# ScalarE copies in layer 0's norms and transforms, and expert inputs prepared two pairs ahead, in a four-layer network

## The chip, the cores and the metric

The kernel runs on one core of one Trainium2 chip. The metric is the device time of one execution in microseconds (us). A core has five engines that each work through their own queue of instructions in order: TensorE (PE: matrix products, with its weight loads shown as PEld), VectorE (DVE), ScalarE (ACT), GpSimd (POOL) and SyncE (SP, which here issues most DMA transfers). They wait for one another by semaphores. Matrix products land in PSUM, in banks of 128 x 512 floats, and an engine other than PE has to read a bank before PE can use it again.

## The reference

Eight samples of 256 channels and 32 x 32 pixels, all in float32, pass through four layers. The parts that the change touches are these:

```python
# layer 0, all of it on (B, 256, 32, 32)
def _ln(x, w, b):                       # the norm ahead of attention and of the feed-forward part
    r = lax.rsqrt(jnp.mean(x * x, axis=1, keepdims=True) + LN_EPS)
    return x * r * w + b
a = _attention(_ln(x, norm1_w, norm1_b), ...)   # softmax attention, 4 heads, plus a depthwise 3x3 of v
x = x + gamma1 * a
f = _edffn(_ln(x, norm2_w, norm2_b), ...)       # 1x1 (pi), depthwise 3x3, gelu(x1) * x2, 1x1 (po),
x = x + gamma2 * f                              # then rfft2 of 8x8 patches * fft_p, irfft2
# layer 1: a bottleneck with a deformable 3x3 convolution
# layer 2: causal attention; then a feed-forward part for the 511 tokens of 1024 with the largest weight
weights = x @ wr + br
_, idx = top_k(weights, 512);  sel = x[idx[:511]]
y = (gelu(sel @ w1 + b1) @ w2 + b2) * weights[sel];  out = x, with y added at the picked rows
# layer 3: attention with squared scores in place of a softmax; then 8 experts, two for each token
probs = softmax(tokens @ router_w.T);  rw, re = top_k(probs, 2)
for e in range(8):
    out += combine[:, e] * (gelu(tokens @ w1[e] + b1[e]) @ w2[e] + b2[e])
```

## The kernel before, in words

**Layers and order.** Six generators, `fast0` to `fast3e` (list LAYERS), give the instructions of layer 0, layer 1, layer 2's attention, layer 2's feed-forward part, layer 3's attention with routing, and layer 3's experts. They run one after the other; each one's first steps are drawn in at the end of the one before by `net.head()`. Inside a layer several streams, one for each sample and stage, are merged by `by_time`: every stream has a start and a spacing in steps, and the one that is due next gives its next step. `spread` does the like in layer 3. A scheduler then may reorder the instructions of an engine where data allow it; an instruction that goes through `net.pinned` keeps its place in program order. Each engine's queue runs in order on the chip, so an instruction that waits holds back everything behind it on its engine.

**Layer 0** (`fast0`, L1110). The main stream is attention, 32 steps a sample (T = 32): a step makes scores s on PE (L1393), exponentials e of 128 x 1024 on ScalarE (L1399), values A on PE (L1357) and the running sum of e on DVE (L1353). Beside it run, for other samples: `before_attention` (norm, q, k, v, depthwise part of v), `before_gates` (the second norm), `gates` (the 1x1 pi, L78 through `net.linear`; its copies to hp by ScalarE, L1434; the depthwise 3x3 as eight DVE steps of about 1.23 us each, L1246; gelu on ScalarE between two loads of its function table, L1459 and L1460) and `transforms` (po, fwd, gain, back: L1487 to L1507, four times a sample). All of these take their PSUM from `bank`, which while attention runs has two banks (tag X) in rotation: PE can use a bank when the engine that reads the one of two before has done so. After attention there are four.

`normed` (L1213) is called twice a sample. For each of the two halves k of the channels ScalarE squares 128 x 1024 (L1218) and PE sums the square over channels into a bank ms (L1220); in `before_gates` both squares use one buffer `sq`, so the second square waits for the first product. ScalarE makes r = rsqrt (L93, L94), PE spreads r over all partitions into two banks rb (L1229), and DVE multiplies x by each of the banks (L1233, 128 x 1024 each). In `transforms`, fwd (L1495) is multiplied by the gain on DVE out of PSUM (L1496).

**Layer 2's feed-forward part** (`fast2f`, L2044). `before(b)` makes the norm xn of a sample by ScalarE, then on DVE eight products with wr (L2116) that yield the column wcol, and an added constant (L2119). PE turns wcol into a row wrow (L2124) by which the tokens are ranked. `place` scatters tokens, `ready` loads the picked ones and turns them (xs, L2178; copied by DVE to xk, L2183), `main` makes h (L78), its gelu, and y (L2200), to which DVE adds b2 (L2207). The DVE instructions L2119 and L2207 are not pinned; in the engine's order, from the third sample on, an addition L2207 of an earlier sample stands between the fifth and the sixth product L2116.

**Layer 3's attention and routing** (`fast3`, `Routes`). `between(b)` runs beside sample b's attention: it routes sample b - 1 and makes the norm and projections of sample b + 1. For b = 0 it first runs `routes.fill`: DVE makes a row of zeros with a destination that is out of bounds, and eight DMAs on SP's queue (L2359) write such rows to the three lists into which tokens will be sorted by expert.

**Experts** (`fast3e`, L2725). The lists are worked in 76 pairs of blocks of 128 rows, in three groups. For pair q: `load` fetches rows xs by DMA, four pairs ahead, into five buffers; `fetch` turns xs on PE (a, L2807) and copies it by DVE to xk (L2809, two buffers); `first` makes h on PE (L2821) and its gelu hid (L2827); `second` converts the rows' destinations (`to`, L2839, POOL, pinned), makes y on PE (L2843), adds b2 on DVE (L2847) and scatters each block by POOL (L1026). Step q issues `first(q)`, `fetch(q + 1)`, `second(q - 1)`. Beside it, `sort` prepares the last group and `combine` adds up the results of finished groups (L2909) and turns them back (oT, L2920).

Of the kernel before, what the change touches and what calls it, by code (L numbers as in the profile page):

```python
# [17 lines left out]
P = 128  # L18
# [1091 lines left out]
def fast0(net, io):  # L1110
# [7 lines left out]
    with ExitStack() as ctx, ExitStack() as att:  # L1118
# [94 lines left out]
        def normed(xn, x, sq):  # L1213

            ps = bank("ms")
            for k in range(KC):
                s_ = sq(k)
                nc.scalar.activation(s_, x[:, k, :], AF.Square)  # L1218
                for h in range(2):
                    nc.tensor.matmul(  # L1220
                        ps[64 * h : 64 * h + 64], lhsT=net.mean64, rhs=s_[:, bass.ts(h, HF)],
                        start=(k == 0), stop=(k == KC - 1),
                    )
            r = one.tile([P, HF], F32, tag="r", name="r")
            net.rsqrt(r, ps, net.eps6)
            yield
            for h in range(2):
                pr = bank("rb")
                nc.tensor.matmul(  # L1229
                    pr, lhsT=net.unit[64 * h : 64 * h + 1, :], rhs=r[64 * h : 64 * h + 1, :], start=True, stop=True  # L1230
                )
                cols = bass.ts(h, HF)
                nc.vector.tensor_tensor(  # L1233
                    xn[:, :, cols], x[:, :, cols], pr.unsqueeze(1).to_broadcast([P, KC, HF]), ALU.mult
                )
# [183 lines left out]
        def before_gates(b):  # L1419
            xn = xs[b] = one.tile([P, KC, N], F32, tag="xn2", name="xn2")  # L1420
            nc.sync.dma_start(out=xn, in_=mids[b])
            yield
            yield from normed(xn, xn, lambda k: one.tile([P, N], F32, tag="sq", name="sq"))
            yield
# [42 lines left out]
        def transforms(b):  # L1467
# [12 lines left out]
            for pr in range(4):  # L1480
# [4 lines left out]
                for pc in range(2):  # L1485
# [10 lines left out]
                nc.vector.tensor_tensor(  # L1496
                    u, ps.rearrange("p (t c) -> p t c", c=C), gain.unsqueeze(1).to_broadcast([P, 2, C]), ALU.mult
                )
# [19 lines left out]
        for b in range(B):  # L1518
            streams += [
                (T * (b - 1) - 2, 32 / 20, before_attention(b)) if b > 1 else (11 * b, 1.0, before_attention(b)),  # L1520
                (T * (b + 1) + 7.5, 1, before_gates(b)),
# [3 lines left out]
        for _ in range(9):  # L1525
            next(streams[1][2])
# [517 lines left out]
def fast2f(net, io):  # L2044
# [5 lines left out]
    with ExitStack() as ctx, ExitStack() as mid:  # L2050
# [26 lines left out]
        def before(b):  # L2077
# [41 lines left out]
            nc.vector.tensor_scalar(wcol, wcol, vec[:, 10:11], None, ALU.add)  # L2119
# [66 lines left out]
        def main(b):  # L2186
# [9 lines left out]
            for t2 in range(0, 4, 2):  # L2196
                ps = bank("y")
                for i in range(2):
# [8 lines left out]
                nc.vector.tensor_tensor(  # L2207
                    y[:, t2 : t2 + 2], ps.rearrange("p (t c) -> p t c", c=C),
                    b2.unsqueeze(1).to_broadcast([P, 2, C]), ALU.add,
# [86 lines left out]
class Routes:  # L2296
# [49 lines left out]
    def fill(self):  # L2346
# [8 lines left out]
        for g, so in enumerate(self.sorteds):  # L2355
            self.fills[g] = []
            for lo in range(0, TILES[g], 26):
# [4 lines left out]
                )  # L2362
                self.fills[g].append(ins.ins)
# [142 lines left out]
def fast3(net, io):  # L2506
# [4 lines left out]
    with ExitStack() as ctx, ExitStack() as tok, ExitStack() as att, ExitStack() as bef:  # L2511
# [175 lines left out]
        def between(b):  # L2687

            if b:
                yield from routes.route(b - 1, xs[b - 1], one, pair)  # L2690
            else:
                yield from routes.fill()
            if b + 1 < B:
                yield from norm(b + 1)
                yield from projections(b + 1)
            else:
# [28 lines left out]
def fast3e(net, io):  # L2725
# [4 lines left out]
    with ExitStack() as ctx:  # L2730
# [9 lines left out]
        five = io.pool(ctx, "f3ec", 5)  # L2740
        psP = io.pool(ctx, "f3ep", 1, PSUM)
# [26 lines left out]
        def experts():  # L2768
            xss, xks, w1s, hids = {}, {}, {}, {}
# [28 lines left out]
            def fetch(q):  # L2798
# [5 lines left out]
                xs, ps = xss[q], bank("a")  # L2804
# [3 lines left out]
                xks[q] = two.tile([P, 2, KC, P], F32, tag="xk", name="xk")  # L2808
                nc.vector.tensor_copy(  # L2809
                    xks[q][:, :n].rearrange("p j k n -> p (j k n)"), ps[:, :n].rearrange("p j c -> p (j c)")  # L2810
                )

# [19 lines left out]
            def second(q):  # L2832
# [4 lines left out]
                hid, xs = hids.pop(q), xss.pop(q)  # L2837
                to = five.tile([P, 2], I32, tag="to", name="to")
                net.pinned(nc.gpsimd.tensor_copy(to[:, :n], xs[:, :n, C]))  # L2839
# [19 lines left out]
            fetch(0)  # L2859
            yield  # L2860
            for q in range(len(pairs)):
# [3 lines left out]
                fetch(q + 1)  # L2865
# [73 lines left out]
        sorting = sum(steps[:-1]) - lead - 2 * AHEAD - 2  # L2939
# [281 lines left out]
```

## Time and profile before

| what | value |
|---|---|
| time, median of three runs (lowest, highest) | 4359.39 us (4353.24, 4366.02) |
| the profiled execution's own time | 4372.2 us |
| its span in the trace | 4370.4 us |
| its mean granted clock of TensorE | 0.948 |
| busy: PE, DVE, ACT, POOL | 4008.9, 2298.0, 2228.2, 564.7 us |
| busy, weight loads (beside PE) | 1944.2 us |
| DMA | 350.34 MB, 80 GB/s in the mean |

A row of the waits names the engine, its operation and line, what ended the idle time before it, and then the total in us, the number and the longest. A row of the timeline has start and duration in us, engine, line, operation, out<-in with partitions x elements, how many such instructions are merged (x), and in brackets the idle time just before the first and what ended it; "issue" and "remote" stand where the profile shows no releasing instruction. A row of stages has the stretch in us, its length, the busy time of each engine with the number of instructions, the granted clock of TensorE (1 is full speed), the DMA engines' busy share and GB/s. The stages in the span are, roughly: layer 0 to 1480, layer 1 to 1950, layer 2's attention to 2450, its feed-forward part to 2980, layer 3's attention to 3960, the experts to 4335, and the last sums to the end.

### The profile page before, as it was taken

The numbers are of one execution on the slowest core, as the hardware profiler recorded it, in microseconds if no ns is written. First come the engines' busy times: TensorE is split into PE (matmuls) and PEld (weight loads), VectorE is DVE, ScalarE is ACT, GpSimd is POOL, SyncE is SP. The second block draws the span as 40 slices with busy tenths as digits, with TensorE's granted clock in tenths as the row PEclk, the third lists the DMA queues.
The fourth block names the chain that finished last, engine by engine and source line by source line (L and its number), as shares of the span: only waits on it lengthen the run. The fifth ranks groups of instructions, "written<-read, shape, count | busy, mean of one in ns | idle before, by whom it ended". The sixth has DMA issues, their size and how long they took to land. (4 is left out here: it accounts for less than half of the span.)

```text
span 4370.4 us, 53086 instructions
## 1 busy us (share of the span) xinstructions
PE 4008.9 (92%) x20006; PEld 1944.2 (44%) x20006; DVE 2298.0 (53%) x3995; ACT 2228.2 (51%) x2966; POOL 564.7 (13%) x645
## 2 busy tenths in 40 slices
PE   8989999999888889989999988889999999998887
PEld 3223333333333444444444435554444444336776
DVE  2387877887886577752222246642332323324345
ACT  3455555555453366643433454425665556665444
POOL 0000000000000000000000013331000150134653
PEclk9988999999898999999999988899999999999998
DMA  2212222222213111110100012346100040145566
GB/s 89 67 59 84 88 74 89 86 76 80 79 47 116 62 42 58 40 43 1 39 20 20 29 48 93 118 145 186 37 30 30 20 127 30 35 132 179 186 211 212
DMA packets 190636, 350.34 MB, mean 80 GB/s; under 512 B 24121, under 2 KB 134668, under 8 KB 178852
## 3 DMA queue, kind: packets, MB, share of 16 engines
q1 hardware_dynamic: 167124, 294.10, 20.8%
q0 software_dynamic: 19440, 46.45, 3.2%
q10 hardware_dynamic: 3808, 6.29, 0.4%
q8 instruction: 162, 2.65, 0.3%
q14 instruction: 102, 0.84, 0.1%
HBM read 175.15 MB, written 153.89 MB: 75 GB/s over the span
## 5 line engine op out<-in xcount | busy, mean ns | idle before, releaser
L1246 DVE SCALAR_TENSOR_TENSOR a<-hp,w_f_vec,a 128x961 f32<-128x961 f32 (+1 forms) x496 | 608.5, 1232 | 154.3 <-ACT a L1239 146.2
L2677 ACT ACTIVATE e<-s,five 128x1024 f32<-128x1024 f32 x512 | 539.2, 1110 | 276.9 <-PE s L2671 260.6
L2671 PE MATMUL s<-q,k 32*128 32x512 f32 x2048 | 349.2, 645 | 7.9 <-DVE cnt L2437 2.0
L78 PE MATMUL pi<-xn,w_l_wpi 128*128 128x512 f32 x512 | 268.1, 670 | 41.5 <-DVE u L1496 31.0
L1399 ACT ACTIVATE e<-s 128x1024 f32<-128x1024 f32 x256 | 249.3, 1020 | 109.0 <-PE s L1393 106.3
L2655 PE MATMUL A<-e,v 128*32 128x512 f32 x2048 | 279.6, 611 | 0.3 <-ACT e L2677 0.3
L1353 DVE TENSOR_TENSOR sum<-sum,e 128x1024 f32<-128x1024 f32 x192 | 230.7, 1218 | 87.6 <-ACT e L1399 87.5
L1357 PE MATMUL A<-e,va 128*32 128x512 f32 x2048 | 268.8, 606 | 0.0
L1434 ACT ACTIVATE hp<-pi,pib 128x512 f32<-128x512 f32 x128 | 87.6, 688 | 229.5 <-PE pi L78 223.4
L1393 PE MATMUL s<-q,k 32*128 32x512 f32 x1024 | 199.4, 664 | 0.2 <-ACT e L1399 0.2
L2821 PE MATMUL h<-xk,w 128*128 128x128 f32 x1192 | 159.2, 290 | 43.1 <-DVE xk L2809 33.7
L78 PEld LDWEIGHTS pi<-xn,w_l_wpi 128*128 128x128 f32 x512 | 104.6, 214 | 199.0 <-issue 118.7
L2671 PEld LDWEIGHTS s<-q,k 32*128 32x128 f32 x2048 | 111.2, 184 | 173.7 <-issue 99.2
L2821 PEld LDWEIGHTS h<-xk,w 128*128 128x128 f32 x1192 | 153.1, 204 | 54.9 <-DVE xk L2809 38.9
L1721 PE MATMUL pos<-pos,w_f_sel 64*128 64x512 f32 x576 | 163.6, 629 | 9.3 <-ACT ax L1732 2.9
L1026 POOL DMA_INDIRECT res<-y,to x149 | 150.1, 1007 | 153.3 <-issue 135.2
L2792 ACT COPY w<-w_l3f_w 128x512 f32 x149 | 92.6, 625 | 138.3 <-PE h L2821 107.3
L1307 POOL MEMSET thrice<- 32x128 f32 x32 | 6.3, 196 | 1085.0 <-PE pe L1324 1062.3
L2843 PE MATMUL y<-w_l3f_w,hid 128*128 x596 | 143.0, 382 | 0.2 <-ACT hid L2827 0.2
L1026 POOL DMA_INDIRECT so<-xl,rows x128 | 129.6, 1012 | 91.7 <-issue 62.0
L1357 PEld LDWEIGHTS A<-e,va 128*32 128x32 f32 x2048 | 58.8, 110 | 175.6 <-issue 175.6
L2584 DVE COPY v<-v 128x1024 f32<-128x1024 f32 x16 | 19.5, 1223 | 217.0 <-PE v L78 217.0
(404 smaller groups left out, 7149.8 us busy)
## 6 DMA issues: line engine op xcount, KB each, us to landing
x<-d SPq DMA_DIRECT2D x31, 1024.0 KB
xs<-so SPq DMA_DIRECT2D x73, 260.0 KB
so<-zero SPq DMA_DIRECT2D x5, 3380.0 KB
thrice<-v SPq DMA_DIRECT2D x256, 64.0 KB
gated<-st SPq DMA_DIRECT2D x32, 512.0 KB
hc<-gated SPq DMA_DIRECT2D x32, 512.0 KB
d<-x SPq DMA_DIRECT2D x16, 1024.0 KB
xl<-mox SPq DMA_DIRECT2D x64, 256.0 KB
```

Source lines behind the costliest of these rows:

```text
L78: self.nc.tensor.matmul(ps, lhsT=w[:, i, m], rhs=src[:, i, cols], start=(i == 0), stop=(i == k - 1))
L1026: made = self.nc.gpsimd.indirect_dma_start(**args)
L1246: nc.vector.scalar_tensor_tensor(to, fr, taps(t_), to, ALU.mult, ALU.add)
L1353: nc.vector.tensor_tensor(half, half, e[j], ALU.add)
L1357: nc.tensor.matmul(state["A"][32 * h : 32 * h + 32, c, :], lhsT=vas[b][:, kt, c, 32 * h : 32 * h + 32], rhs=e[h // 2][:, h % 2, :], start= ...
L1393: nc.tensor.matmul(ss[h // 2][:, h % 2], lhsT=ks[b][32 * h : 32 * h + 32, bass.ts(kt, P)], rhs=qs[b][32 * h : 32 * h + 32, bass.ts(gq, HF) ...
L1399: nc.scalar.activation(es[i][j], ss[j], AF.Exp, scale=SCALE)
L1721: nc.tensor.matmul(ps[:, bass.ts(h, HF)], lhsT=sel[r, t, xy, :], rhs=poss[b][r, :], start=True, stop=True)
L2655: nc.tensor.matmul(A[32 * h : 32 * h + 32], lhsT=v[:, kt, c * P + 32 * h : c * P + 32 * h + 32], rhs=e[:, h, :], start=first, stop=last,)
L2671: nc.tensor.matmul(ss[h // 2][:, h % 2], lhsT=k[32 * h : 32 * h + 32, c, bass.ts(kt, P)], rhs=q[32 * h : 32 * h + 32, c, bass.ts(hh, HF)], ...
L2677: nc.scalar.activation(e[:, 2 * j : 2 * j + 2], ss[j], AF.Square, scale=SCALE, bias=five)
L2821: nc.tensor.matmul(ps[:, j, m], lhsT=ws[j][:, k, bass.ts(m, P)], rhs=xk[:, j, k], start=(k == 0), stop=(k == KC - 1),)
```

## The change

1. In `normed` both squares are made before the products, into two buffers (in `before_gates` the second takes a buffer of tag `a`), with a step of the stream in between. The two rb banks are copied by ScalarE into the first square's buffer, and one DVE multiply of 128 x 2048 in SBUF takes the place of two of 128 x 1024 out of PSUM. In `transforms` ScalarE copies fwd's bank to u, and DVE multiplies u by the gain in SBUF. The streams' starts and spacings are adapted to the added step.
2. In `fast2f` the additions L2119 and L2207 are pinned. In the changed kernel's order on DVE the eight products L2116 and L2119 now come together, and then L2207 and the copy to xk.
3. `routes.fill` moves behind the norm and the projections of sample 1, and its DMAs are pinned.
4. In `fast3e`, xk has three buffers, step q issues `fetch(q + 2)`, the conversion `to` moves into `fetch`, so that xs is given back there, and the sort stream's spacing is made for two steps fewer.

```diff
@@ fast0, normed
+            squares = [sq(k) for k in range(KC)]
+            for k in range(KC):
+                nc.scalar.activation(squares[k], x[:, k, :], AF.Square)
+            yield
             ps = bank("ms")
             for k in range(KC):
-                s_ = sq(k)
-                nc.scalar.activation(s_, x[:, k, :], AF.Square)
                 for h in range(2):
                     nc.tensor.matmul(
-                        ps[64 * h : 64 * h + 64], lhsT=net.mean64, rhs=s_[:, bass.ts(h, HF)],
+                        ps[64 * h : 64 * h + 64], lhsT=net.mean64, rhs=squares[k][:, bass.ts(h, HF)],
...
-                cols = bass.ts(h, HF)
-                nc.vector.tensor_tensor(
-                    xn[:, :, cols], x[:, :, cols], pr.unsqueeze(1).to_broadcast([P, KC, HF]), ALU.mult
-                )
+                nc.scalar.copy(squares[0][:, bass.ts(h, HF)], pr)
+            nc.vector.tensor_tensor(xn, x, squares[0].unsqueeze(1).to_broadcast([P, KC, N]), ALU.mult)
@@ before_gates
-            yield from normed(xn, xn, lambda k: one.tile([P, N], F32, tag="sq", name="sq"))
+
+            def square(k):
+                return five.tile([P, N], F32, tag="a", name="sq") if k else one.tile([P, N], F32, tag="sq", name="sq")
+
+            yield from normed(xn, xn, square)
@@ transforms
-                nc.vector.tensor_tensor(
-                    u, ps.rearrange("p (t c) -> p t c", c=C), gain.unsqueeze(1).to_broadcast([P, 2, C]), ALU.mult
-                )
+                nc.scalar.copy(u.rearrange("p t c -> p (t c)"), ps)
+                nc.vector.tensor_tensor(u, u, gain.unsqueeze(1).to_broadcast([P, 2, C]), ALU.mult)
@@ streams of layer 0
-                (T * (b - 1) - 2, 32 / 20, before_attention(b)) if b > 1 else (11 * b, 1.0, before_attention(b)),
-                (T * (b + 1) + 7.5, 1, before_gates(b)),
+                (T * (b - 1) - 2, 32 / 21, before_attention(b)) if b > 1 else (11 * b, 1.0, before_attention(b)),
+                (T * (b + 1) + 7.4, 0.9, before_gates(b)),
...
-        for _ in range(9):
+        for _ in range(10):
@@ fast2f
-            nc.vector.tensor_scalar(wcol, wcol, vec[:, 10:11], None, ALU.add)
+            net.pinned(nc.vector.tensor_scalar(wcol, wcol, vec[:, 10:11], None, ALU.add))
...
-                nc.vector.tensor_tensor(
-                    y[:, t2 : t2 + 2], ps.rearrange("p (t c) -> p t c", c=C),
-                    b2.unsqueeze(1).to_broadcast([P, 2, C]), ALU.add,
+                net.pinned(
+                    nc.vector.tensor_tensor(
+                        y[:, t2 : t2 + 2], ps.rearrange("p (t c) -> p t c", c=C),
+                        b2.unsqueeze(1).to_broadcast([P, 2, C]), ALU.add,
+                    )
                 )
@@ Routes.fill
+                self.net.pinned(ins)
                 self.fills[g].append(ins.ins)
@@ fast3, between
-            else:
-                yield from routes.fill()
             if b + 1 < B:
                 yield from norm(b + 1)
                 yield from projections(b + 1)
+                if b == 0:
+                    yield from routes.fill()
@@ fast3e
+        three = io.pool(ctx, "f3ek", 3)
...
-                xs, ps = xss[q], bank("a")
+                xs, ps = xss.pop(q), bank("a")
...
-                xks[q] = two.tile([P, 2, KC, P], F32, tag="xk", name="xk")
+                xks[q] = three.tile([P, 2, KC, P], F32, tag="xk", name="xk")
...
+                to = tos[q] = five.tile([P, 2], I32, tag="to", name="to")
+                net.pinned(nc.gpsimd.tensor_copy(to[:, :n], xs[:, :n, C]))
...
-                hid, xs = hids.pop(q), xss.pop(q)
-                to = five.tile([P, 2], I32, tag="to", name="to")
-                net.pinned(nc.gpsimd.tensor_copy(to[:, :n], xs[:, :n, C]))
+                hid, to = hids.pop(q), tos.pop(q)
...
             fetch(0)
+            fetch(1)
             yield
             for q in range(len(pairs)):
                 weights(q + 1)
                 first(q)
                 yield
-                fetch(q + 1)
+                fetch(q + 2)
...
-        sorting = sum(steps[:-1]) - lead - 2 * AHEAD - 2
+        sorting = sum(steps[:-1]) - lead - 2 * AHEAD - 4
```

More of the change, by code (lines that the diff above doesn't have):

```diff
@@ L2768, in experts @@
         def experts():
[L2769 removed]
+            xss, xks, w1s, hids, tos = {}, {}, {}, {}, {}
             def load(q):
```

## Prediction

> **What bounds the kernel now.** I read the busy shares by stage first, to see which engine sets the time and where it has room.
>
> ```profile
> core 0: us, PE busy (x) PEld busy (x) DVE busy (x) ACT busy (x) POOL busy (x), PEclk, DMA share, GB/s
> 0.00:1480.00 1480.00, 1339.76 (x6225) 519.58 (x6226) 1037.03 (x1005) 729.23 (x917) 13.35 (x49) 0.92 0.25 79
> ...
> 2450.00:2980.00 530.00, 448.25 (x1566) 273.98 (x1565) 280.04 (x935) 220.33 (x331) 145.76 (x143) 0.90 0.32 102
> 2980.00:3960.00 980.00, 968.40 (x5750) 395.49 (x5749) 297.39 (x833) 610.38 (x611) 173.69 (x165) 0.99 0.21 67
> 3960.00:4335.00 375.00, 329.91 (x2218) 304.22 (x2217) 175.26 (x424) 186.82 (x464) 203.05 (x269) 0.95 0.61 195
> ```
>
> TensorE (PE) is busy in nearly all of every stage and no other engine comes near it. So the time is PE's work, plus its idle stretches, plus what it loses at a granted clock below 1. Only the last two can be won: 140 us of idle in layer 0 (1480 - 1339.8), 82 in the picked-token FFN, 45 in the experts, but only 12 in layer 3's attention. Next, the view of waits, PE's rows only, says who ends the idle.
>
> ```profile
> PE h L2821 <- DVE xk L2809: 33.7, 16, 6.4
> PE pi L78 <- DVE u L1496: 31.0, 8, 5.0
> PE wrow L2124 <- DVE wcol L2119: 21.1, 4, 9.2
> PE ms L1220 <- ACT sq L1218: 19.9, 9, 6.2
> PE fwd L1495 <- DVE xn L1233: 18.1, 4, 4.5
> ...
> PE xn L2564 <- DVE xt L1019: 9.0, 1, 9.0
> PE pi L78 <- DVE xn L1233: 8.8, 4, 7.8
> ...
> PE wrow L2124 <- issue: 4.8, 1, 4.8
> ```
>
> These are total us, number, longest. Every row is a place that the diff touches. Then the timeline, one stall of each sort, and the granted clock of single stretches (seventh figure).
>
> ```profile
> 432.39 1.28 ACT L1459 ACT_TABLE_LOAD   x1
> 433.69 2.19 ACT L1459 ACTIVATE st<-a 128x512 f32<-128x512 f32 x4
> 435.90 1.28 ACT L1460 ACT_TABLE_LOAD   x1
> ...
> 440.07 0.68 DVE L1496 TENSOR_TENSOR u<-fwd,w_l_gam 128x512 f32<-128x512 f32 x1
> ...
> 440.81 5.40 PE L78 MATMUL pi<-xn,w_l_wpi 128*128 128x512 f32 x8 [3.77 <-DVE u L1496]
> ```
> ```profile
> 372.73:389.80 17.07, 16.43 (x32) 5.45 (x33) 6.94 (x7) 6.00 (x8) 0.00 (x0) 0.50 0.44 161
> ...
> 2779.13:2789.37 10.24, 3.42 (x16) 3.45 (x17) 2.12 (x8) 1.43 (x2) 1.89 (x2) 0.50 0.39 76
> ```
> ```profile
> 2783.43 0.69 DVE L2207 TENSOR_TENSOR y<-y,w_f_b 128x512 f32<-128x512 f32 x1 [9.48 <-remote]
> ...
> 2785.57 0.23 DVE L2119 TENSOR_SCALAR wcol<-wcol,w_l2f_vec 128x8 f32<-128x8 f32 x1
> ```
> ```profile
> 4183.17 0.69 DVE L2809 COPY xk<-a 128x512 f32<-128x512 f32 x1 [8.61 <-remote]
> ...
> 4183.92 3.78 PE L2821 MATMUL h<-xk,w 128*128 128x128 f32 x16 [6.45 <-DVE xk L2809]
> ```
>
> In layer 0 a PSUM bank is emptied by DVE, which comes to it 3 us late behind its own queue. In the FFN the add of y (L2207) stands among the instructions that make wcol, so wcol and PE behind it wait for it. In the experts PE waits for one copy, xk.
>
> **Part 1, layer 0.** Removed: 32 DVE multiplies out of rb's PSUM (L1233, 1214 ns) and 32 out of fwd's (L1496, 683 ns). Added: the same multiplies from SBUF (rb's in pairs, one of 128x2048; by 2 x 1214 about 2.4 us) and 64 ScalarE copies of 128x512. The nearest row for those is va's copy L1298, 584 ns, so 64 x 0.584 = 37 us more ScalarE, from 729 to 766 of 1480. DVE's sum stays. What is won is not work but the time at which a bank comes free.
>
> A rule speaks against this: the Trainium skill, "ScalarE: Activation LUTs", Rules for kernel authors, gives elementwise work such as add and mul to VectorE and not to ScalarE; a copy is of that kind. By the rule these copies are 37 us of added work with nothing won, so layer 0 gains only from the squares, about 9. By the rows the ScalarE copy is as quick (584 against 683 ns), and the delay is DVE's queue, 70% full against ScalarE's 49%. I go by the rows, within limits: ScalarE's queue is in order as well.
>
> Site by site. *pi behind u*, 31.0 in 8: the copy can't run before the chain of gelu is past (1.28 + 2.19 + 1.28 = 4.75 us in the order of the changed kernel), with the exponentials (1.02 each) mixed in. ScalarE was free of the chain at 437.2, PE waited from 437.0, so the copy ends between 437.8 and 440.4 and leaves 0.8 to 3.4 of the 3.8. I take 2.6: 8 x 1.2 = 9 won. *fwd behind xn*, 18.1 in 4: six depthwise steps of 1.25 us stood ahead on DVE; PE waits from 490.2, and rb's copy could end between 490.1 (ScalarE's next instruction) and 492.6 (behind one tile's two exponentials), so 0 to 2.4 is left; I take 2.4, as at the site before: 4 x 2.1 = 8 won. *pi behind xn*, 8.8: 5 won. *ms behind sq*, 19.9 in 9: both squares are now issued a step ahead and into two tiles, but the first still waits for the load of xn (372.27): 9 won. With 2 for smaller rows that is 33 of about 80.
>
> Clock: 30 stretches at 0.5 lie in layer 0, 249 us together; about 180 of these are busy (estimate: 249 less some 70 of idle), which lost 90. Here a second rule is to be weighed: "TensorE: Matmul & The Clock Gate", The HAM clock gate, has the clock fall after an idle window of about 3.4 us. By that, the short stalls of 1.95 us at ms cost only themselves. The row at 372.73 shows 17 us at half clock, 16.4 of it busy, around just such a stall: 8.2 lost besides. By the rule the shortened stalls, all under 3.4 now, would return most of the 90; by the row a stall of 2 us can still cost as much as one of 4. I take 16, a sixth.
>
> New waits: xn is whole after two copies and one multiply (1.2 + 2.4 = 3.6 us), where its halves were ready after 1.2 and 2.4: 1.8 later in the mean, 16 times; vT's and D's banks now wait for copies behind exponentials; the second square takes one of the five buffers of `a`, which a depthwise image of the sample before must have left (what stands behind it on ScalarE are exponentials, and PE behind them). All is hidden where attention's tiles stand between; all uncovered, 16 x 1.8 = 29. I take half, 14. Sum of part 1: -33 - 16 + 14 = **-35**, with ends of about -100 (all idle and two thirds of the covered clock loss back) and +70 (see the rivals).
>
> **Part 2, sums in order.** No work is added or taken: in the changed order DVE makes wcol at once, then y's add, then xk's copy. The five gaps before wrow are 21.1 + 4.8 and 3.3 (put down to DVE junk), 29 in all; one of 3.9 has no y add ahead and stays: 25 can go. At the clock the row at 2779 loses 3.4/2 = 1.7, times four 7. Top: -32. But y's add started at 2783.4 although y's last matmul ended at 2776.7 by the record, and I can't say why. If it stays so late, h waits next, since xk's copy (1.23) stands behind y's add (0.69): PE first has wrow 1.9, xs 1.9 and y 1.7, so of 6.7 + 1.9 about 3 remain, at the two longest stalls: 25 - 6 + 4 = -23 at the bottom, or -10 if h's wait takes most of it. I take **-25**.
>
> **Part 3, zero rows.** Eight DMAs (page: 3380 KB, x5 recorded, so about 17 MB) go behind the loads of samples 1 and 2 and some stores on SP's queue. The 9.0 us stall of xn at 2941 had DVE's preparation of the zero rows (four instructions, some 3.7 us) and a wait of 2.5 for a load in it: **-3**, at most -9. What is late next is whatever follows the fills on SP: stores of routed rows and loads for sorting. The cover is the 968 of 980 busy us of attention; without it, one more stall of 9, so +9 at worst.
>
> **Part 4, experts.** The copy xk is made two pairs ahead. A pair's PE work is h 1.78 + a 0.44 + y 1.73 = 3.96 us (chain of waits), so each of the 16 waits gets 3.96 more cover: the 6.4 leaves 2.5, the others nothing: 33.7 - 2.5 = 31. At the clock some 31 us at half lie here, perhaps 24 busy, 12 lost: 4 back. Moved: 76 copies of `to` on POOL (0.2 us each) go ahead of the scatters of pair q-1. They wait for the load of the pair two ahead, and behind them in POOL's order stand scatters (1.0 us) and with those y's buffers. POOL is busy 203 of 375, so 0 where the load has landed; at the two group borders I allow 2 each: +4. The sort stream is shorter by two steps of about 85: nothing. **-31**, ends -45 and 0. The tail after 4335 waits for other things and stays.
>
> **Sum.** -35 - 25 - 3 - 31 = -94. The profiled execution took 4372.2 (span 4370.4), 13 above the median of the three runs, 0.3%. I take the difference over: 4359.4 - 94 = **4265**.
>
> **Rivals.**
> *Stalls only move in layer 0* (chance 0.25): PE waits for ScalarE's copies as long as for DVE's. For it: the 4.75 us chain; against: ScalarE's 51% idle. Then 4359 - 59 = 4300. If the expert stage too is bound by its transfers (195 GB/s, DMA share 0.61, against: a share well below 1), 4331.
> *Nearly all comes back* (0.14): -80 in layer 0, -32, -5, -40, so 4202. For it: stalls under 2 us that pass without the clock falling; against: the row at 372.73.
> *Slower* (0.05): the 32 fwd copies wait for the whole gelu chain while both of the rotating banks are full, so PE stands 4.75 - 0.68 = 4.1 longer at each: 131 - 59 = +72, 4431. From 1.8 us a copy on it outweighs the other parts. Against it: one chain for four copies of a sample at most.
> *No change* (0.06): all but a few of the stalls reappear at the next wait.
>
> **Chances.** The forecast as told, 4230 to 4290, has 0.5. The range, 4205 to 4335, takes in the first rival with its worse end and the near edge of the second; no change and slower are left out. Faster by over 0.3% (13 us, about what a measurement of this kernel can tell from no change) 0.90, within 0.05, slower 0.05.
>
> **What would show it.** Right: wrow<-wcol falls to one wait of about 4, h<-xk below 6, pi<-u gone with a row pi or back<-ACT u of some 20 in its place, PE's clock in layer 0 at 0.93 to 0.94. Wrong: waits for ACT's copies of 40 or more, half-clock stretches as many as before, h<-xk in the FFN above 10, or a new PE wait in the experts for xs or for y's scatters.

## The result and the profile after

The changed kernel takes 4318.2 us in the median of four runs (4310.4 to 4324.1), the kernel before, beside it on the same chip, 4362.4 (4353.2 to 4366.0). The ratio is 0.9907, 95% interval 0.9881 to 0.9933: 44 us faster, where 94 had been forecast. 4318 lies inside the range of 4205 to 4335 and outside the likeliest case of 4230 to 4290. The profiled execution has a span of 4321.1 us against 4370.4, so the traces hold 49 to explain.

To compare stages that end at other times, I cut both traces at the same instructions of PE: the first product c of layer 1, qk of layer 2, h of the picked-token stage, xn of layer 3, a of the experts, and the last h. The last sample's feed-forward part of layer 0 still runs beside layer 1 after the first of these cuts. The rows below are stages (stretch and length, busy us of PE, PEld, DVE, ACT and POOL with the number of instructions, granted clock, DMA share, GB/s): layer 0, the picked-token stage, layer 3's attention and the experts, first in the kernel before, then in the changed one.

```profile
0.00:1320.10 1320.10, 1201.39 (x5786) 454.78 (x5786) 948.62 (x894) 675.67 (x832) 13.35 (x49) 0.92 0.25 78
2637.60:2941.40 303.80, 260.33 (x964) 178.23 (x964) 177.27 (x669) 130.83 (x206) 109.57 (x113) 0.91 0.35 111
2941.40:3956.70 1015.30, 1001.59 (x5869) 416.72 (x5869) 314.32 (x860) 614.83 (x615) 186.30 (x176) 0.99 0.24 75
3956.70:4333.10 376.40, 329.94 (x2221) 304.24 (x2222) 178.56 (x435) 185.79 (x462) 201.45 (x268) 0.95 0.61 197
```
```profile
0.00:1294.50 1294.50, 1182.66 (x5786) 447.21 (x5786) 945.60 (x879) 703.48 (x886) 13.36 (x49) 0.96 0.25 80
2613.20:2904.40 291.20, 260.00 (x965) 175.33 (x965) 177.66 (x669) 130.77 (x206) 109.68 (x113) 0.94 0.36 116
2904.40:3926.70 1022.30, 1002.00 (x5868) 416.09 (x5868) 314.93 (x859) 614.62 (x615) 186.43 (x178) 0.99 0.24 74
3926.70:4283.40 356.70, 329.32 (x2222) 303.14 (x2222) 174.84 (x435) 183.00 (x462) 200.06 (x268) 0.96 0.64 209
```

| stage, cut at the same instructions | before | after | gained | forecast |
|---|---|---|---|---|
| layer 0 | 1320.1 | 1294.5 | 25.6 | 35 |
| layers 1 and 2's attention, up to the first h | 1317.5 | 1318.7 | -1.2 | 0 |
| picked-token stage | 303.8 | 291.2 | 12.6 | 25 |
| layer 3's attention | 1015.3 | 1022.3 | -7.0 | 3 |
| experts | 376.4 | 356.7 | 19.7 | 31 |
| last sums | 37.3 | 37.7 | -0.4 | 0 |

PE's waits in the changed kernel, in the columns of the same view before:

```profile
PE y L2203 <- issue: 17.9, 19, 1.7
PE back L1506 <- DVE u L1501: 13.2, 13, 4.0
PE D L1372 <- ACT v L1234: 12.3, 6, 2.3
PE s L2677 <- ACT e L2683: 12.1, 2, 11.2
...
PE pe L1324 <- DMA thrice<-v: 11.3, 9, 2.1
...
PE pi L78 <- ACT u L1500: 9.2, 6, 1.5
PE h L2830 <- DVE xk L2816: 9.1, 4, 5.4
...
PE wrow L2127 <- DVE wcol L2122: 3.9, 1, 3.9
```

Each of the five big waits has gone or shrunk as the diff meant it to (h behind xk 33.7 to 9.1, wrow 21.1 to 3.9, ms behind sq 19.9 to 7.2, pi and fwd 49 to 9). But rows have come in at other places: D and pi behind ScalarE's copies, back behind DVE's multiply, y behind nothing that the profile shows, and one single wait of 11.2 us. PE's idle fell by 31 us in the whole span, from 361 to 330.

### The profile page after: what moved, and what is told of

Same layout as the page of the kernel before. It is cut to its first block, busy times and chain, and to the rows that moved or that the text cites. A ratio compares the mean times of both kernels' runs of the same rounds, so it can differ in the third digit from the quotient of the medians.

```text
span 4321.1 us, 53170 instructions
## 1 busy us (share of the span) xinstructions
PE 3991.1 (92%) x20006; PEld 1934.1 (45%) x20006; DVE 2293.2 (53%) x3979; ACT 2258.6 (52%) x3030; POOL 563.1 (13%) x645
## 5 line engine op out<-in xcount | busy, mean ns | idle before, releaser
L2677 PE MATMUL s<-q,k 32*128 32x512 f32 x2048 | 350.9, 644 | 16.6 <-ACT e L2683 12.1
L78 PE MATMUL pi<-xn,w_l_wpi 128*128 128x512 f32 x512 | 247.3, 625 | 14.3 <-ACT u L1500 9.2
L1393 PE MATMUL s<-q,k 32*128 32x512 f32 x1024 | 183.9, 649 | 2.2 <-ACT e L1399 2.2
L78 PEld LDWEIGHTS pi<-xn,w_l_wpi 128*128 128x128 f32 x512 | 95.9, 197 | 155.1 <-issue 118.1
L1324 PE MATMUL pe<-thrice,w_f_wpe 96*32 96x496 f32 (+1 forms) x768 | 129.1, 606 | 18.1 <-DMA thrice<-v 11.3
L2203 PE MATMUL y<-w_l2f_w,hid 128*128 128x256 f32 x512 | 125.3, 401 | 17.9 <-issue 17.9
```

Source lines behind the costliest of these rows:

```text
L78: self.nc.tensor.matmul(ps, lhsT=w[:, i, m], rhs=src[:, i, cols], start=(i == 0), stop=(i == k - 1))
L1393: nc.tensor.matmul(ss[h // 2][:, h % 2], lhsT=ks[b][32 * h : 32 * h + 32, bass.ts(kt, P)], rhs=qs[b][32 * h : 32 * h + 32, bass.ts(gq, HF) ...
L2677: nc.tensor.matmul(ss[h // 2][:, h % 2], lhsT=k[32 * h : 32 * h + 32, c, bass.ts(kt, P)], rhs=q[32 * h : 32 * h + 32, c, bass.ts(hh, HF)], ...
```

## The experiments

My theory after the result: the change does remove the stalls, but a part of what they cost is due at once to the next wait. The rivals: the four parts disturb one another, or the missing half lies in one part that costs time. Except where it is said, all kernels start from the changed one. They ran in five groups, each on another chip, with the kernel before beside them. The kernel before took 4362 us in the first comparison and 4363 and 4376 in two of the groups, but 4291 to 4297 in the other three. So times are compared inside a group or as ratios to the kernel before, and stages by the trace. A stage's length comes from one trace of each kernel; layer 0 of the changed kernel, for one, took 1288 to 1295 us in the ten traces that leave it as it is, so a few us in one pair mean little.

### Each part undone

```diff
undo_layer0: squares, ScalarE copies, stream starts and spacing as before
undo_ffn:    the two net.pinned(...) of fast2f removed
undo_fill:   routes.fill() at the start of between(0), not pinned
undo_expert: fetch(q + 1), two buffers xk, `to` in second, as before
```

> The changed kernel with layer 0 as it was before (squares, ScalarE copies and stream spacing undone). Theory (each part's share is what its own stage shows between the two traces; parts do not interact): layer 0 to the first product of layer 1 takes 1320 us again instead of 1294.5, later stages stay as in the changed kernel, time about 4318 + 25 = 4343. Rival (layer 0's part is worth the 35 of the prediction, and something later gave 10 back because it came earlier): 4353, with a later stage shorter than in the changed kernel.

> The changed kernel without the two pinned additions in the picked-token stage. Theory: the stalls of wrow on wcol return (five, 28 us together) and PE's short waits before y (16 us in the changed kernel) fall to about 7, so the stage is 13 us longer, 4331. Rival (the pins alone are worth the 25 of the prediction and the rest is lost elsewhere for another reason): the stage is 25 longer, 4343.

> The changed kernel with the zero rows written at the start of layer 3 again and not pinned. Theory: moving them cost time, because eight fills in a row hold up a store of routed rows and the load of the next sample on SP's queue; the 11.2 us wait of s for e at about 3121 goes, the 2.5 us wait of kT returns, time 4318 - 7 = 4311. Rival (the 11.2 us wait has another cause, such as the earlier arrival in layer 3): the wait stays and the time is 4318 to 4322.

> The changed kernel with the expert inputs prepared one pair ahead again. Theory: the experts take 376 us from the first a to the last h again instead of 357, 16 or so waits of h for xk of 34 us together return, time 4337. Rival (the expert stage is 11 short of the prediction because another part disturbs it): with the old order the stage takes 365 to 370, not 376.

| kernel | ratio to before (95%) | us | what its stage shows | the same stage in the other three |
|---|---|---|---|---|
| undo_layer0 | 0.9950 (0.9932 to 0.9969) | 4356.8 | layer 0: 1312.2 | 1289.1 to 1292.7 |
| undo_ffn | 0.9913 (0.9890 to 0.9937) | 4335.9 | picked-token stage: 298.7 | 300.2 to 300.8 |
| undo_fill | 0.9876 (0.9855 to 0.9897) | 4318.6 | layer 3's attention: 1012.9 | 1022.3 to 1029.8 |
| undo_expert | 0.9946 (0.9926 to 0.9966) | 4354.2 | experts: 382.0 | 351.8 to 361.2 |

The changed kernel itself did not run in this group, so the last column is the mark. Layer 0 (some 21 us) and the experts (some 25) did about as the theory had it. For the picked-token stage both theory and rival missed: without the pins it took 298.7 us, with them 300.2 to 300.8. The 12.6 us of the first pair don't come back, so nothing shows that the pins made them; in the seven traces with pins on chips of this sort the stage took 291.2 to 300.8, and the first pair had the shortest. Here is what took the place of the wrow stalls, PE's rows of the timeline in the changed kernel (first pair):

```profile
2750.26 1.06 PE L2181 MATMUL xs<-ident,xs 128*128 128x128 f32 x8
...
2752.45 0.38 PE L2203 MATMUL y<-w_l2f_w,hid 128*128 128x256 f32 x1 [0.69 <-issue]
2753.87 0.38 PE L2203 MATMUL y<-w_l2f_w,hid 128*128 128x256 f32 x1 [1.05 <-issue]
```
```profile
2756.94 1.22 DVE L2186 COPY xk<-xs 128x1024 f32<-128x1024 f32 x1 [7.86 <-remote]
```

The DMA engines' busy tenths in slices of 0.5 us, from 2744 on:

```profile
DMA  0040079399999999999895993300000000000003
```

wrow no longer waits, and PE goes on, but then y's products come one at a time, and xs, whose products ended at 2751.3 by the record, is given to DVE at 2756.9 only, when a burst of DMA ends. Before, it was y that was given late, and PE stood at wrow. (Below I call a semaphore late that is raised well after the product that it tells of has ended.) There is a delay in both; the pins only moved the place where PE meets it.

undo_fill did as its theory had it, and is the fastest of the four. The single 11.2 us wait goes with the move of the zero rows, and one of 2.8 us at kT is back. In the changed kernel SP's queue and the engines behind it read:

```profile
3044.35 50.70 SPq L2364 DMA_DIRECT2D so<-zero  x8
3095.15 5.24 SPq L2382 DMA_DIRECT2D mox<-mo_x  x1
...
3112.33 0.33 SPq L2561 DMA_DIRECT2D x<-d  x1
...
3119.34 0.43 DVE L1003 BATCH_NORM_STATS2 tn_s<-x 128x6 f32<-128x256 f32 x1 [15.46 <-DMA x<-d]
3119.89 0.30 ACT L1008 ACTIVATE tn_r<-tn_m,eps 128x8 f32<-128x8 f32 x1 [11.81 <-DVE tn_m L1006]
...
3121.48 2.07 PE L2677 MATMUL s<-q,k 32*128 32x512 f32 x4 [11.18 <-ACT e L2683]
```

Eight fills, now in a row, hold SP for 50.7 us; the stores of routed rows and the load of the next sample come behind. That load is issued 168.6 us after the first s, where it was 137.5 before. Two small ScalarE instructions of the norm wait for it, and the exponentials of attention stand behind them on ScalarE's queue, and PE behind those.

### What in layer 0 does it

```diff
squares_only: both nc.scalar.copy undone, DVE multiplies out of PSUM; the rest of layer 0 as changed
no_fwd_copy:  only the copy of fwd undone
spacing20:    -(T * (b - 1) - 2, 32 / 21, before_attention(b))  +(..., 32 / 20, ...)
```

> The changed kernel with both kinds of ScalarE copies undone: rb and fwd are multiplied by DVE out of PSUM as before, while the two squares ahead of their products, the added step and the spacing stay. Theory (the copies turn stalls of 4 us that let the clock fall into stalls of 1 to 2 that don't): the waits pi<-u and fwd<-xn return with some 50 us, layer 0 is 1294 + 18 = 1312 us long, time about 20 above the changed kernel on the same chip. Rival (the squares and the spacing brought the gain, since ms<-sq fell from 17 to 5): layer 0 stays at 1295 to 1300.

> The changed kernel with the fwd copy alone undone (rb is still copied by ScalarE). Theory: the wait pi<-u of about 30 us returns with half-clock stretches behind it and layer 0 is some 10 longer, 1303 to 1306. Rival (ScalarE's chain of gelu delays the copy as much as DVE's queue did): within 3 of the changed kernel, 1289 to 1295.

> The changed kernel with the spacing of before_attention as before (32/20 in place of 32/21), the added step kept. Theory: in the changed kernel the fourth group of pe products of each sample comes only 12 us after the third and waits for its load of v (3.5 us a sample, partly hidden in busy time, some 20 in all); with the wider spacing this goes and layer 0 is 10 to 15 shorter, 1280. Rival (the groups are moved elsewhere and other waits come in): 1290 to 1300.

Ratios to the kernel before on that chip: 1.0016 (1.0002 to 1.0029), 1.0009 (1.0001 to 1.0018), 0.9864 (0.9848 to 0.9881). From the start to the first c they took 1315.7, 1320.6 and 1265.6 us; layer 0 as changed took 1295.4 on that chip (in ffn_no_gather, below). The row of spacing20:

```profile
0.00:1265.60 1265.60, 1146.44 (x5788) 452.17 (x5788) 949.87 (x880) 702.79 (x886) 13.39 (x49) 0.96 0.26 82
```

The kernel before took 1314.5 to 1320.1 in its traces. So the squares ahead and the new spacing together give 4 us at most; rb's copies added to that give none; and the fwd copy, added last, brings 1320.6 to 1295.4, more than the 10 that I had expected of it. In no_fwd_copy pi behind u is back with 34.0 us in 12. The fwd copy leaves 1.5 us where 3.8 were: in the changed kernel it ran right behind the gelu chain, ahead of the exponentials.

```profile
438.55 1.28 ACT L1464 ACT_TABLE_LOAD   x1
439.84 0.59 ACT L1500 COPY u<-fwd 128x512 f32<-128x512 f32 x1
...
440.32 1.95 ACT L1399 ACTIVATE e<-s 128x1024 f32<-128x1024 f32 x2
...
440.48 1.98 PE L78 MATMUL pi<-xn,w_l_wpi 128*128 128x512 f32 x4 [1.53 <-ACT u L1500]
```

And the new spacing cost some 30 us (1295.4 to 1265.6; 24 in the pair after_again and best, below). The fourth group of pe products is 24 in one piece before (first row); in the changed kernel it looks like the rows after that:

```profile
455.32 2.71 PE L1324 MATMUL pe<-thrice,w_f_wpe 96*32 96x512 f32 x24
```
```profile
455.33 1.02 PE L1324 MATMUL pe<-thrice,w_f_wpe 96*32 96x512 f32 x2
456.89 1.02 PE L1324 MATMUL pe<-thrice,w_f_wpe 96*32 96x512 f32 x2 [0.54 <-DMA thrice<-v]
457.84 0.70 PE L1491 MATMUL po<-w_l_wpo,hc 128*128 128x256 f32 x2
458.47 1.05 PE L1324 MATMUL pe<-thrice,w_f_wpe 96*32 96x512 f32 x2
459.45 1.13 PE L1491 MATMUL po<-w_l_wpo,hc 128*128 128x256 f32 x4
460.51 2.71 PE L1324 MATMUL pe<-thrice,w_f_wpe 96*32 96x512 f32 x18
```

In the kernel before the products run four abreast: in the single records four start within 0.02 us (455.32 to 455.34), each takes 0.59 us, and the next four start 0.43 us after the first. In the changed kernel the first six run alone, two in 1.02 us (0.43 + 0.59), and the second and third pair each wait for another load of v, as do the 18 that follow, which run three or four abreast. So the 24 take 5.8 us, and in the busy column this counts as work. With 32/20 they run in one piece (3.06 us at 447). My theory had the cause, loads of v that are only just under way, but put it at 10 to 15, and took the loss for waits inside busy time, where it is products that run one by one. Over the layer pe's products take 18 us less busy time than in ffn_no_gather, and 9 more is time at half clock (17 and 2 in the other pair).

The groups of 5.8 us stand in squares_only and no_fwd_copy as well, since these keep 32/21, and there pe takes 23 and 16 us more than in the kernel before. So what the squares are worth without that spacing was not measured, and the 4 us are no measure of them: PE's waits of over 3.4 us fell from 68 us in all to 34 in squares_only (26 in the changed kernel), and its time at half clock from 203 to 127 (107), while the layer stayed as long as it was.

With 32/20 another thing shows, by the row of spacing20: PE's idle time is 1265.6 - 1146.4 = 119 us, as much as the 118.7 before the change. The layer is 55 us shorter than in the first trace, and all of it is busy time, 1201.4 to 1146.4, at a granted clock of 0.96 in place of 0.92. (Against before_third, below, on a like chip, it is 49, with idle up by 3.)

### The picked-token stage on other chips

```diff
ffn_no_gather(2): after(b): no indirect_dma_start; yg is one buffer of zeros
ffn_no_load:      before(b): for b >= 2 no load of x, the tile of sample 1 is used again
ffn_quiet(2):     both
```

> The changed kernel with the picked-token stage's gathers left out (the eight indirect loads of y per sample; the addition on DVE stays and reads a buffer of zeros, so layer 2's output lacks the picked part). Theory (PE's short waits before y or xs, 16 us, and the late semaphores of y and xs come from bursts of DMA, of which the gathers are a part, and set the stage): these waits fall below 5 and the 291 to 301 us from the first h to layer 3's first product fall by 10 or more. Rival (they come from the place in the instruction stream): the waits stay at 12 to 16 and the stage stays within 5.

> The changed kernel with the picked-token stage's gathers of y left out (a buffer of zeros is added in their place), once more, beside a kernel that has them on the same chip. Theory (bursts of DMA hold PE's completions back): where the fourth kernel of this job shows 15 to 25 us of waits before y and xs, this one shows 10 or less, and the stage from the first h to layer 3's first product is 8 or more shorter. Rival (the waits come from the place in the instruction stream): 15 to 25 here as well.

> The changed kernel with the loads of x for samples 2 to 7 of that stage left out (the tokens of sample 1 are worked again in their place). Theory: the same, with fewer bytes in the burst: waits before y and xs fall by a third or more. Rival: they stay.

> Both left out. Theory: waits before y and xs of 5 or less, the stage 260 to 270 us, as on the chip that showed no such waits. Rival: 15 to 25 us, 290 or more.

> The changed kernel with gathers and loads of x left out of the picked-token stage. On a chip with late semaphores, theory (DMA bursts hold PE's completions back): waits before y and xs of 5 or less and a stage of 260 to 275 us. Rival (something else on these chips does): 13 to 25 us of such waits and 290 or more. On a chip without: 258 as in the last job.

> The kernel before. On a chip without late semaphores, theory (the stalls of wrow behind y's addition exist only because y's semaphore is late): no wrow stall but the first of 3.9, the stage from the first h to layer 3's first product 255 to 265 us as in the changed kernel there (259 to 261), and the experts 340 to 350 (changed: 336 to 341). Rival (order alone makes them): wrow stalls of 10 us or more, the stage 270 or more. On a chip with late semaphores: 299 to 304 and 376 to 379 as before.

With these runs the bursts could not be judged. On the chips on which they ran, the waits before y and xs were absent in every kernel: 184 to 186 us from the first h to the last wrow in all (212.1 in the first trace, 213.8 on a third chip with these waits), whether the gathers and loads were there or not. The stage took 257.1 to 260.4 us in the five kernels that leave transfers out, and 259.4 to 261.2 in those that have them all. So the five tell nothing of how a burst and a late semaphore hang together. What they led to was the kernel before on such a chip:

```profile
PE h L2821 <- DVE xk L2809: 12.8, 5, 4.8
...
PE h L2821 <- DVE bey_o L2972: 7.0, 1, 7.0
...
PE wrow L2124 <- DVE wcol L2119: 4.4, 3, 3.9
```
```profile
2636.00:2898.60 262.60, 248.27 (x964) 168.84 (x964) 176.33 (x669) 130.16 (x206) 109.53 (x113) 0.97 0.41 128
3909.10:4258.20 349.10, 325.87 (x2222) 304.23 (x2223) 178.53 (x435) 185.92 (x462) 200.63 (x268) 0.95 0.65 213
```

The same kernel, the same order of instructions, and the four big wrow stalls are not there: 4.4 us in place of 29, and the experts' 33.7 is 12.8. The stage takes 262.6 us; with the pins it took 259.4 to 261.2 on such chips. The experts take 349.1; with two pairs ahead 336.2 to 341.2.

The kept traces say more. Each records when a semaphore was raised. I counted those of PE that came over 1.5 us after the last finished product that can have raised them. In the picked-token stage these are 7 to 10 in each of the ten traces on chips of the first sort (in the kernel before 8, the latest 10.2 us behind), and none in the ten on the others; in the experts 7 to 33 against none. ScalarE has none in these stages, DVE three at most. As events are missing from those traces, the counts are lower bounds.

The DMA engines do much the same on both sorts of chip. In the picked-token stage they were over 0.85 busy for 49 us in the first trace of the kernel before, 8.0 at a time at most, and for 51 us and 9.0 in before_third. A packet of the queue of indirect transfers took 125 ns in the mean in the first trace and 127 in before_third, one of SP's queue 91 and 92, and one that brings instructions, on two queues, 1026 and 470 against 1131 and 454. So neither slower transfers nor slower loading of instructions explain the delay, and a burst alone does not make one. What differs between the chips was not found. One suspect was not tested, the recording itself: where semaphores are late, the trace lacks events too (in the picked-token stage 277 of the 339 of DVE are there and 100 of the 130 of ScalarE, while in layer 0 none is missing), and every run here has a recorded span.

### Two traces on one chip, and a faster version

```diff
before_again, after_again: the two kernels as they are
best:        32 / 20 in place of 32 / 21, and routes.fill() where it was before
best_no_rb:  best, with rb multiplied by DVE out of PSUM
best_between: best_no_rb, with routes.fill() between norm(1) and projections(1)
```

> The kernel before, profiled on the same chip as the three kernels after it. In the last two experiments PE's short waits before y and xs in the picked-token stage were gone in all kernels, with the gathers or without. Theory (whether semaphores of PE arrive late in that stage and in the experts is a property of the chip, not of the kernel): if this chip has no such waits in the changed kernel, then the stalls of wrow on wcol are gone here too or below 5 us, and the stage from the first h to layer 3's first product is 260 to 270 us in this kernel as well. Rival (the pins removed the stalls and the other edits only moved the burst): here the wrow stalls are 20 to 30 us and the stage 295 to 305.

> The changed kernel on the same chip. Theory: layer 0 takes 1294 us as on the first chip (the kernel before 1320), the move of the zero rows costs 7 to 9, and what the picked-token stage and the experts gain is that much smaller as this chip shows fewer late semaphores: 0 to 5 and 5 to 15 where there are none. Ratio 0.990 to 0.996 in that case, 0.990 otherwise. Rival: all parts give the same as on the first chip, 0.990.

> The changed kernel with the spacing 32/20 and the zero rows where they were before. Theory (both effects add): layer 0 1265 us, layer 3's attention 967 instead of 983, so 29 + 9 = 38 shorter than the changed kernel, ratio to the kernel before about 0.982. Rival (the wait of the next sample's load returns by another way, or the first stage's gain is taken back): 25 or less shorter than the changed kernel.

> The same without the ScalarE copies of rb (only fwd is copied by ScalarE). Theory (the fwd copies bring the gain and rb's copies bring none: with the squares alone layer 0 took 1316 us, with rb's copies added 1321, with fwd's added too 1294): within 5 us of the kernel with them, to either side. Rival (with fwd's banks free early, DVE's late multiply from rb is the next stall): 10 to 20 longer, with fwd<-xn or D<-xn waits of 15 or more.

> The fastest kernel so far (fwd copies, squares ahead, spacing 32/20, pins, experts two pairs ahead) with the eight zero-row DMAs between the norm and the projections of sample 1, where SP's order has them ahead of two of the sums' stores and of the load of sample 2. Theory (a burst of fills late is what holds the next sample's load): neither the 2.5 us wait of kT nor the 11 us wait of s for e shows, and the ratio is 0.978 to 0.981. Rival (either place costs one of the two): 0.981 to 0.984.

| kernel | ratio to before (95%) | layer 0 | picked-token stage | layer 3 | experts |
|---|---|---|---|---|---|
| before_again | - | 1314.5 | 299.1 | 1010.7 | 378.6 |
| after_again | 0.9917 (0.9893 to 0.9941) | 1288.1 | 298.0 | 1029.4 | 356.3 |
| best | 0.9829 (0.9804 to 0.9853) | 1264.0 | 295.7 | 1018.6 | 353.1 |
| best_no_rb | 0.9806 (0.9782 to 0.9831) | 1270.1 | 297.0 | 1013.5 | 357.0 |
| best_between (another chip) | 0.9881 (0.9858 to 0.9903) | 1268.0 | 261.2 | 1027.7 | 340.3 |

This chip had late semaphores, and on it the pins gained 1 us in the stage (299.1 to 298.0), while 22 us of stalls at wrow and 8 before y became 4 at wrow and 24 before y and xs. Layer 3 lost 19 us here. Both corrections add, as the theory had it: best is 39 us, 0.9 points, below the changed kernel. The copies of rb bring nothing clear: without them the time is 7 us less, and layer 0 6 us longer. best_between ran on a chip without late semaphores, where the kernel before is faster, so its ratio is to be set beside the 0.9864 of spacing20. It fell short: kT waits 3.2 us and s another 10.6, for DVE xn this time, and DVE for the load of the next sample. So both later places of the zero rows cost a stall of over 10 us, and the old one has only 2.7 at kT. Why the load of best_between comes too late, though it is issued as early as in best (16 us and 17 after the first s), was not looked into.

## Why the prediction was wrong

Most of the named stalls went as worked out, and still the forecast is 53 us off, because two terms were mis-sized and two steps failed. That the picked-token stage gave 12.6 in the first pair was luck: elsewhere the same edit gave 3 at most.

**Layer 0, forecast 35, measured 25.6.** The step "with 2 for smaller rows that is 33 of about 80", less 14 for new waits, failed as a sum: idle fell from 118.7 to 111.8 us only, by 7. The single stalls shrank as worked out or better (pi behind u 1.5 left, I took 2.6; D 2.3 in fwd's place, I took 2.4), but there are more of them: D, vT, back, pi behind ScalarE. The clock gave more than the 16 that I took. By the clock's records PE had 203 us at half speed before and 107 after; 173 and 97 of these were busy, so (173 - 97) / 2 = 38 came back. And a loss that no step named, the spacing 32/21, took 24 to 30, nearly all as busy time. I had read the spacing as an adaptation to the added step and costed it at nothing, without naming the cover: the distance between two pe groups and the load of v between them. So the mechanism, banks that come free sooner, was there, but it paid through the clock and hardly through less idle time. Two figures of this part were wrong besides: of the 249 us at half clock 208 were busy and not 180, and the end of -100 does not come out of its terms (all of 80 idle and two thirds of 90 make 140, less 14 of new waits).

The two rules that I weighed: ScalarE's copies did pay for fwd (25 us), where DVE's queue was long, and brought nothing for rb. That the length of the two queues decided is my reading; no run varied it alone. On the clock, the truth lay between the row and the page (the Trainium skill, "TensorE: Matmul & The Clock Gate", The HAM clock gate): 38 us came back, where I took 16 by the row and the page's rule would have returned most of 90. These are rows of the changed kernel, around a stall of 1.5 us (at 440.5) and one of 2.3 (at 501.0):

```profile
436.00:446.00 10.00, 7.99 (x41) 3.60 (x41) 9.80 (x11) 8.53 (x12) 0.00 (x0) 1.00 0.29 105
...
500.00:506.00 6.00, 5.05 (x29) 1.67 (x30) 5.93 (x5) 2.61 (x5) 0.00 (x0) 0.72 0.00 1
```

The clock stayed full at all six stalls of 1.5 us of pi behind u; at the five of 2.3 before D it fell in four, mostly for one step of 3.4 us (the granted clock is the third figure from the end). But it fell behind a wait of 1.5 us at 105.2 too. So stalls well below the 3.4 us of idle that the page states can cost clock in this trace, and no clean limit can be read from it; still, with fewer waits above 3.4 us (68 us in all before, 26 after) the time at half clock was about halved.

**The picked-token stage, forecast 25, measured 12.6 in this pair and 1 on another chip.** The step "25 can go" failed. I had noted that y's semaphore came 6.7 us after its products (10.2 after those that the addition waits for: they ended at 2773.3, and 2776.7 is the end of the next bank's) and could not say why, and took the waits as made by the order of DVE's instructions. The kernel before on a chip without late semaphores shows no such stall with the same order, and with late ones the pins leave the stage as long as it was. So the lateness was the cause and the order only the place; why semaphores come late stays open. What was "late next" was named wrongly as well: I expected h behind xk, and it was y and xs, with no releaser shown.

**The zero rows, forecast 3 gained, measured 7 lost.** Both halves of the step failed. The 9.0 us wait of xn stayed at 9.0 after the preparation of the rows had left it, so that did not make it. And the cover "968 of 980 busy us of attention" was no cover for what stands behind the fills: a load that ScalarE's queue needs has PE behind it within a few steps. I had put this at one stall of 9, "at worst"; it was one stall of 11.2, less 2.5 won at kT and some 2 at small waits. (The eight DMAs move 19.4 MB, not 17: beside the five of 3380 KB stand one of 1690 and two of 390.)

**The experts, forecast 31, measured 19.7.** The term was mis-sized. h behind xk fell by 24.6 and not by 31; 5.4 of the 9.1 us left are one wait, in which DVE stood for a load of the range check that follows the layers:

```profile
4165.46 0.42 DVE L2977 TENSOR_SCALAR_CACHE_REDUCE bey_j<-bey_s 128x256 f32<-128x256 f32 x1 [8.60 <-DMA bey_s<-sums]
```

That is an instruction from outside the stage in DVE's queue, and PE waited for this check once before the change too (2.2 us). Waits with no releaser before h, y and a took 6 more than before. Where semaphores are not late the part is worth 8 to 13.

The rival that came nearest was "stalls only move", which I had tied to layer 0 alone, at 4300. It held in the picked-token stage, and there because of late semaphores; in layer 0 the idle time did move, and the gain came through the clock.

## What to carry to other kernels

A stall that follows a semaphore which itself comes late is not made by the order of the waiting queue: ask first why it is late, since a new order only changes where the engine meets the delay. A change of spacing or place "to fit" is an edit with a price; cost it by the distance between a load and its use and by what stands behind it on its queue, and try the old value with the new code (here 24 to 30 us and 9). An experiment that takes one part out keeps the side effects of the others: squares_only kept the spacing, and so could not price the squares. And a loss can hide in busy time, in products that run one by one where four could run abreast as in a slower clock: compare the length of one group of products, not the busy share.

## What the hardware showed that was not expected

Chips differ in a way that a profile shows. In the first comparison and in two groups of runs PE's semaphores arrived 2 to 10 us late in the two stages with most DMA (busy shares of 0.35 and 0.61), PE's products came one at a time with no releaser named, and the picked-token stage took 291 to 304 us; on the chips of the other three groups none of this appeared, the stage took 257 to 263, and the kernel before was about 70 us faster (4291 to 4297 against 4362 to 4376), 68 of them in these two stages by the traces. In the first trace the longest waits end with a burst of DMA, but like bursts pass without a delay on the other chips, so the cause stays open. The ratio of the whole change was measured on chips of the first sort alone. On the second the gain would be about 24 us, an estimate from the stages (layer 0 25, picked tokens 2, experts 10 gained, layer 3 13 lost); the five kernels that only leave transfers out took 4260 to 4271 us there, 20 to 32 less than the kernel before.
